# When the stored weight sums, the gathers, the token count and a residual step are issued in a conditioned block

## The chip, the cores and the metric

The kernel runs on one core of one Trainium2 chip. The metric is the device time of one execution in microseconds. A core has five engines with a queue each, which run side by side and wait for one another through semaphores: TensorE (PE in the profile; its weight loads are PEld), VectorE (DVE), ScalarE (ACT), GpSimd (POOL) and SyncE (SP). DMAs are issued from the queues of SP, ACT and POOL. Each queue is in order: what an engine waits for also holds up everything behind it on that engine.

## The reference

32 sequences of 128 tokens with 512 features, a condition vector for each sequence, and a mask. The block is computed in float32:

```python
emb = silu(t) @ ada_w + ada_b                       # per sequence: shift, scale, gate_msa
norm = layernorm(x) * (1 + scale) + shift
norm = where(m, norm, 0)
fwd = gelu(norm @ ssm_w1 + ssm_b1) @ ssm_w2 + ssm_b2
bwd = flip(gelu(flip(norm) @ bwd_w1 + bwd_b1) @ bwd_w2 + bwd_b2)
x = x + gate_msa * where(m, fwd + bwd, 0)           # changes the tokens with m only
ff_ada = silu(t) @ ffada_w + ffada_b                # shift_mlp, scale_mlp, gate_mlp
h = gelu_tanh((layernorm(x) * (1 + scale_mlp) + shift_mlp) @ ff_w1 + ff_b1)
out = x + gate_mlp * (h @ ff_w2 + ff_b2)
```

The mask is true for the tokens behind a sequence's end: between 0 and 32 of the 128 in each sequence. Only those go through the first half (the lines with `ssm` and `bwd`). All 4096 tokens go through the second half (`ff`).

## The kernel before

**First half.** The masked tokens get 512 slots, in four tiles of 128 (`NS`, `NH` = 256). `tokens_of` finds the token of each slot, and POOL gathers its row with an indirect DMA (`gather_slots`, tiles `xc`). A matmul with `pick` spreads the condition's rows over the slots (`slot_part(at, j, ...)`: j is 0 for shift, 1 for scale, 2 for gate). `modulated` normalises, scales and shifts on VectorE; `hidden` is the first matmul with its gelu on ACT, `project` the second. `keep_gate` copies a gate tile from PSUM to SBUF on ACT. `keep_slots` adds the bias, multiplies by the gate and adds the old row (three VectorE operations), and SP stores the 128 rows into `x1_rows` in HBM. Slots 0 and 1 are done in the opening (`h1` with name `s0`). Slots 2 and 3 have one `hidden` (`s1`, L1148) and then a `project` each, with names `s2` and `s3` (L1165, L1166).

**Token count.** L638 to L656 count the masked tokens and set `start_at`, `more_i` and `col_l`. They are read only at the very end, where a loop treats masked tokens that did not fit into the slots.

**Second half.** The 4096 tokens go in `NP` = 4 pairs of two sides, a side having `G` = 4 sequences. `x_of[p]` holds the rows of a pair in four SBUF tiles, loaded by `load_side` on SP. `take_first_half` then lays the results of the first half over the masked rows: one indirect DMA on POOL for each sequence, from `x1_rows` by `slot_i`; rows without a slot are left alone. `Statistics.one` takes mean and variance of one sequence on VectorE, `root` the inverse root on POOL, `normalised` applies both. Side 0 of a pair is then transposed in 32x32 blocks on VectorE and put in place by 16 DMAs from SP and ACT (`turned`), and ACT applies scale and shift (`scaled`). Side 1 of pair 0 is transposed on TensorE instead (`transposed`, called by `turn(k)`): four transpositions into one PSUM bank of `ps_t`, which has two, and four VectorE operations that empty it with scale and shift. The four turns lie between the matmuls of `project(1, ...)` for slots 3.

Both matmuls of the second half are done by Strassen's scheme (in Winograd's form), with products P1 to P7 of blocks, where blocks of weights and tokens are first added or subtracted. `FirstProduct` does that at two levels: the inner sums of the weights, `t_sum[1]` to `t_sum[4]`, are formed by `weight_sums` on VectorE in tiles that are wanted again later, stored into `t_rows` in HBM by `store_weight_sums`, and loaded back for each pair by `load_weights` into the tiles `tw`. Each sum is 896 KB, in two DMAs. `t_sum[1]` lies in the two tiles `spare`, into which `load_side(1, 0, spare)` later loads side 0 of pair 1; `t_sum[3]` lies in the tile that next holds the normalised rows of side 0; `t_sum[4]` lies where the sums of the token blocks (`TokenBlocks.one`) are formed next.

**Order.** All of this stands in a `manual_schedule`: each engine runs its instructions in the order in which the code issues them, and only the waits are added. Around the change the order is: slots 0 and 1, store of the sums 3, 1, 2 (L620), the modulation of the second half with its transposition `modT` (L623 to L635), token count, sum 4 and its store (L664, L665), load of side 0 of pair 1 (L1128), six gathers (L1131), the copy of the gate rows to HBM on POOL (L1133), statistics and root of side 0, two gathers, normalisation and `turned`, statistics and root of side 1, slots 2, slots 3 with the four turns, and then the first products with their block sums.

Of the kernel before, what the change touches and what calls it, by code (L numbers as in the profile page):

```python
# [9 lines left out]
F32 = mybir.dt.float32  # L10
I32 = mybir.dt.int32
# [3 lines left out]
ALU = mybir.AluOpType  # L15
# [7 lines left out]
def kernel(  # L23
# [49 lines left out]
    nc = tc.nc  # L73
    B, S, D = x.shape
    P = 128
    assert S == P
    G = 4
# [4 lines left out]
    NS = 512  # L82
    NH = NS // 2
# [6 lines left out]
    const = ctx.enter_context(tc.tile_pool(name="const", bufs=1))  # L90
# [53 lines left out]
    w2 = ssm.tile([P, HC, D], F32, name="w2")  # L144
# [37 lines left out]
    def hidden(xT, n, w, bcol, func, name, pool, parts=range(HC)):  # L182

        h = []
        for f in parts:
            ph = ps_h.tile([P, 512], F32, tag="h", name=f"ph_{name}_{f}")
            for k in range(KC):
                nc.tensor.matmul(  # L188
                    ph[:, :n], w[:, k, ts(f, P)], xT[:, k, :], start=(k == 0), stop=(k == KC - 1)
                )  # L190
            t = pool.tile([P, n], F32, tag="h", name=f"h_{name}_{f}", bufs=HC + 2)
            nc.scalar.activation(t, ph[:, :n], func, bias=biasT[:, bcol + f : bcol + f + 1])  # L192
            h.append(t)
        return h

    def project(i, h, w, name, between=None):

        po = ps_o.tile([P, 512], F32, tag="o", name=f"po_{name}_{i}")
        for f in range(HC):
            if between and f in between:  # L200
                between[f]()
            nc.tensor.matmul(po, h[f][:, ts(i, P)], w[:, f, :], start=(f == 0), stop=(f == HC - 1))  # L202
        return po
# [205 lines left out]
    slot_col = const.tile([P, NC], F32, name="slot_col")  # L409
# [22 lines left out]
    count = const.tile([B, 1], BF16, name="count")  # L432
# [4 lines left out]
    for j in range(2):  # L437
# [4 lines left out]
            start=True,  # L442
            stop=True,
# [139 lines left out]
            }[j]()  # L583
            nc.vector.tensor_tensor(sum_block(j, n), x, y, ALU.subtract)

    def store_weight_sums(*which):
        for j in which:
            nc.sync.dma_start(t_rows[j - 1, :, :4], t_sum[j][0])
            nc.sync.dma_start(t_rows[j - 1, :, 4:], t_sum[j][1][:, :3])


    h1 = []
    gs = []
    xn_s = []
    for c in range(2):
        h1 += hidden(xT_s, NH, w1, 0, AF.Gelu, "s0", ssm, range(4 * c, 4 * c + 3))
        rows = slot_part(2 + c, 1, ps_o, "o"), slot_part(2 + c, 0, ps_o, "o")
        gs.append(keep_gate(c, slot_part(c, 2, ps_o, "o")))
        xn_s.append(modulated(xc[2 + c], *rows, f"s{2 + c}", xn[:, 2 + c]))
        if c == 0:  # L600
# [16 lines left out]
    nc.vector.tensor_scalar(modb_f[B : 2 * B], modb_f[B : 2 * B], 1.0, None, ALU.add)  # L617
    finish_slots(1, h1, gs[1])

    store_weight_sums(3, 1, 2)  # L620

    mod2 = const.tile([3 * B, D], F32, name="mod2")
    pm = ps_o.tile([P, 512], F32, tag="o", name="pm_f")  # L623
# [10 lines left out]
        )  # L634
    nc.vector.tensor_copy(modT.rearrange("p k c -> p (k c)"), ptr[:, : KC * 3 * B])  # L635


    pt = ps_t.tile([P, 512], F32, tag="tr", name="pt")  # L638
    for j in range(2):
        nc.tensor.matmul(pt[:, j : j + 1], every[:, j], count, start=True, stop=True)  # L640
    totals = const.tile([P, 2], F32, name="totals")
    nc.vector.tensor_copy(totals, pt[:, :2])
    total = totals[:, 0:1]
    start_at = const.tile([P, 1], F32, name="start_at")
    nc.vector.tensor_scalar(
        start_at, totals[:, 1:2], float(NH), -float(NS - NH), ALU.is_gt, ALU.mult
    )
    nc.vector.tensor_scalar(start_at, start_at, float(NS), None, ALU.add)
    more_f = const.tile([P, 1], F32, name="more_f")
    nc.vector.tensor_tensor(more_f, total, start_at, ALU.subtract)  # L650
    nc.vector.tensor_scalar(more_f, more_f, float(P - 1), 0.0, ALU.add, ALU.max)
    more_i = const.tile([P, 1], I32, name="more_i")
    nc.vector.tensor_copy(more_i, more_f)
    nc.vector.tensor_scalar(more_i, more_i, 7, None, ALU.logical_shift_right)
    col_l = const.tile([P, 1], F32, name="col_l")
    nc.vector.tensor_scalar(col_l, slot_col[:, 0:1], start_at, None, ALU.add)  # L656

    of_x = {}

    fb2_step = const.tile([P, D // 2], F32, name="fb2_step")  # L660
# [1 line left out]
    t = in_blocks(sp.tile([P, G, D], F32, tag="s12", name="tw_4"))  # L662
    t_sum[4] = [t[:, :4], t[:, 4:]]
    weight_sums(4)  # L664
    store_weight_sums(4)  # L665


    def take_first_half(p, xs, which=range(2 * G)):
        slots = NH if p == 0 else NS
        for i in which:  # L670
            b = 2 * p * G + i
            nc.gpsimd.indirect_dma_start(  # L672
                out=xs[i // G][i % G // 2][:, i % 2],
                out_offset=None,
                in_=x1_rows[:slots, :],
                in_offset=bass.IndirectOffsetOnAxis(ap=slot_i[:, b : b + 1], axis=0),
                bounds_check=slots - 1,
                oob_is_err=False,
            )
# [445 lines left out]
                self.finish(c, 1, 0, a)  # L1125
                self.store(c, 1)

    x_of[1] = [load_side(1, 0, spare)]  # L1128


    take_first_half(0, x_of[0], range(G + 2))  # L1131
    gate_rows = dram.tile([B, D], F32, name="gate_rows")
    nc.gpsimd.dma_start(gate_rows, mod2[2 * B : 3 * B, :])  # L1133
    stats = [Statistics(x_of[0][side], f"0_{side}") for side in range(2)]
    xT = [new_xT(0, side) for side in range(2)]
    for i in range(G):
# [316 lines left out]
```

## Time and profile before

| | us |
|---|---|
| median of 3 runs | 468.26 |
| lowest and highest of them | 466.21, 471.18 |
| the profiled execution | 466.71 |
| its span | 465.0 |
| TensorE busy in it | 449.4 |
| VectorE busy | 331.4 |
| ScalarE busy | 175.0 |
| GpSimd busy | 157.3 |

The granted TensorE clock was 0.998 of full speed. A busy share is a mean over stages with different limits, so it tells little of one place; in the stretch from the first slots' stores (54 us) to the end of the first product's start (114 us) the engines have to be read in order of time. In a line of the timeline the first number is the start in microseconds from the beginning of the span, the second the duration; then come engine, line, operation, output and input. The brackets at the end hold the time for which the engine was idle before it, and what ended that wait. In a table of stretches each engine has its busy microseconds and, in brackets, its instructions; the last columns are the granted clock, the busy share of the 16 DMA engines, and GB/s.

### The profile page before, as it was taken

How to read it: one execution, taken by the hardware profiler on the slowest of the kernel's cores; microseconds unless marked ns; L12 is line 12 of the kernel's file. 1: busy time of each engine (PE TensorE's matmuls, PEld its weight loads, DVE VectorE, ACT ScalarE, POOL GpSimd, SP SyncE). 2: the span in 40 equal slices, each digit the busy share in tenths (PEclk: the TensorE clock that was granted, in tenths of full speed). 3: DMA queues.
4: the chain of work that ended last, by engine and by line, in shares of the span. 5: the costliest groups of instructions: out<-in, count | busy, mean ns of one | idle time of the engine just before them, and what ended most of it. 6: DMA issues, size and time to landing. Idle time of an engine off the chain costs nothing.

```text
span 465.0 us, 5826 instructions
## 1 busy us (share of the span) xinstructions
PE 449.4 (97%) x2000; PEld 364.3 (78%) x2000; DVE 331.4 (71%) x538; ACT 175.0 (38%) x380; POOL 157.3 (34%) x151
## 2 busy tenths in 40 slices
PE   6899998899999999999999999999999999999995
PEld 2475384477888888888888888888888878888884
DVE  4639767899678749986787399867863995434645
ACT  3122020634454371353554613444446144562000
POOL 6200063038972000489710005897000025660000
PEclk9999999999999999999999999999999999999999
DMA  8999893362408653923087348230963342222022
GB/s 277 386 407 355 329 346 68 65 235 64 160 0 209 98 101 100 335 77 147 1 221 105 83 136 320 87 111 3 231 100 78 125 170 78 81 75 107 0 78 107
DMA packets 82482, 70.41 MB, mean 151 GB/s; under 512 B 63168, under 2 KB 63696, under 8 KB 81426
## 3 DMA queue, kind: packets, MB, share of 16 engines
q1 hardware_dynamic: 67586, 57.95, 40.3%
q0 software_dynamic: 4256, 10.75, 6.9%
q10 hardware_dynamic: 10608, 1.32, 2.1%
q8 instruction: 17, 0.28, 0.3%
q14 instruction: 15, 0.12, 0.1%
HBM read 56.83 MB, written 13.17 MB: 151 GB/s over the span
## 4 chain that ended last, share of the span: by engine, by line
PE 63%; DVE 13%; POOL 6%; ACT 6%; issue 6%; SPq 5%; DMA 1%; POOLq 0%; DVEq 0%; ACTq 0%
PE a_m L904 15%; PE a_o L1084 14%; PE e_o L1084 12%; PE e_m L904 12%; SPq L743 5%; PE po_s L202 4%; PE ph_s L188 3%; DVE xn L716 1%; ACT xT L726 1%; ACT hb L866 1%; POOL x L672 1%; DVE sx L833 1%; POOL hb L988 1%; POOL rstd L710 1%; DVE xn_sy L837 1%
## 5 line engine op out<-in xcount | busy, mean ns | idle before, releaser
L955 POOL TENSOR_TENSOR ha<-p_m,ha 128x512 f32<-128x512 f32 x20 | 26.8, 1342 | 152.4 <-ACT ha L962 143.3
L1084 PE MATMUL e_o<-fw,ha 128*128 128x256 f32 x256 | 57.9, 379 | 0.0
L726 ACT ACTIVATE xT<-xT,modT 128x128 f32<-128x128 f32 x112 | 43.8, 480 | 31.4 <-DMA xT<-xn 31.4
L1084 PE MATMUL a_o<-t,hb 128*128 128x256 f32 x240 | 54.1, 379 | 0.0
L1084 PEld LDWEIGHTS e_o<-fw,ha 128*128 128x128 f32 x256 | 48.6, 190 | 6.6
L1084 PEld LDWEIGHTS a_o<-t,hb 128*128 128x128 f32 x240 | 45.6, 190 | 6.2
L672 POOL DMA_INDIRECT x<-x_rows,slot_i x32 | 37.0, 1155 | 26.2 <-DMA x_rows<-t_s 17.9
L866 ACT ACTIVATE hb<-hb,biasT 128x256 f32<-128x256 f32 x64 | 29.0, 501 | 27.8 <-POOL hb L988 19.4
L955 POOL TENSOR_TENSOR hb<-p_m,hb 128x512 f32<-128x512 f32 x20 | 27.7, 1384 | 21.5 <-DVE hb L934 21.1
L918 ACT COPY p_m<-e_m 128x512 f32<-128x512 f32 x27 | 15.8, 586 | 48.2 <-PE e_m L904 45.4
L1084 PE MATMUL e_o<-fw,s 128*128 128x256 f32 x128 | 29.2, 381 | 0.5 <-DVE s L1038 0.3
L962 ACT COPY ha<-e_m 128x512 f32<-128x512 f32 x32 | 18.5, 579 | 29.1 <-PE e_m L904 24.1
L1084 PE MATMUL a_o<-fw,ha 128*128 128x256 f32 x128 | 28.9, 379 | 0.0
L1084 PE MATMUL a_o<-t,s 128*128 128x256 f32 x128 | 28.9, 379 | 0.0
L188 PE MATMUL ph_s<-xT_s,w 128*128 128x256 f32 x128 | 28.7, 382 | 0.0
L202 PE MATMUL po_s<-w,h_s 128*128 128x512 f32 x64 | 28.6, 592 | 0.0
L1084 PEld LDWEIGHTS e_o<-fw,s 128*128 128x128 f32 x128 | 24.1, 190 | 4.8 <-DVE s L1038 1.7
L188 PEld LDWEIGHTS ph_s<-xT_s,w 128*128 128x128 f32 x128 | 24.0, 190 | 4.7 <-ACT h_s L192 1.5
L1084 PEld LDWEIGHTS a_o<-t,s 128*128 128x128 f32 x128 | 24.3, 190 | 3.3
L1084 PEld LDWEIGHTS a_o<-fw,ha 128*128 128x128 f32 x128 | 24.3, 190 | 3.3
L866 ACT ACTIVATE ha<-e_m,biasT 128x256 f32<-128x256 f32 x48 | 20.1, 469 | 15.3 <-PE e_m L904 12.2
L929 DVE TENSOR_TENSOR e_m<-a_m,ha 128x512 f32<-128x512 f32 x20 | 13.9, 697 | 16.1 <-POOL ha L955 6.6
(205 smaller groups left out, 868.8 us busy)
## 6 DMA issues: line engine op xcount, KB each, us to landing
tw<-t_rows SPq DMA_DIRECT2D x16, 896.0 KB, 5.4
x<-in_x_dram SPq DMA_DIRECT2D x16, 512.0 KB, 12.0
gate<-gate_rows POOLq DMA_DIRECT2D x8, 1024.0 KB
out_dram<-x SPq DMA_DIRECT2D x15, 512.0 KB, 3.4
xT<-xn SPq DMA_DIRECT2D x92, 64.0 KB, 2.3
fw<-in_L_cond_ff_w_dram SPq DMA_DIRECT2D x2, 2048.0 KB
ada_f<-in_L_cond_ffada_w_dram SPq DMA_DIRECT2D x4, 768.0 KB
ada_a<-in_L_cond_ada_w_dram SPq DMA_DIRECT2D x4, 512.0 KB, 3.8
```

Source lines behind the costliest of these rows:

```text
L188: nc.tensor.matmul(ph[:, :n], w[:, k, ts(f, P)], xT[:, k, :], start=(k == 0), stop=(k == KC - 1))
L202: nc.tensor.matmul(po, h[f][:, ts(i, P)], w[:, f, :], start=(f == 0), stop=(f == HC - 1))
L672: nc.gpsimd.indirect_dma_start(out=xs[i // G][i % G // 2][:, i % 2], out_offset=None, in_=x1_rows[:slots, :], in_offset=bass.IndirectOffse ...
L726: nc.scalar.activation(out, src, AF.Identity, bias=shift, scale=scale)
L743: queues[b % len(queues)].dma_start(dst[ts(q, R), b], src[ts(b, R), q])
L866: nc.scalar.activation(dst[:, n], src[:, n], AF.Gelu_apprx_tanh, bias=biasT[:, f : f + 1])
L904: nc.tensor.matmul(bank[:, ts(n, QT)], self.w_block(j, product)[:, ts(n, P)], self.x_block(j, product), start=(product in ("P1", "P5") and ...
L918: nc.scalar.copy(p5, e)
L929: nc.vector.tensor_tensor(e, a, p5, add)
L955: nc.gpsimd.tensor_tensor(self.place(RESULT[j], c), self.p5[j], other, ALU.add)
L962: nc.scalar.copy(self.place(RESULT[j], c), src)
L1084: nc.tensor.matmul(part, src[:, k, ts(i, P)], w[product][:, k, :], start=(last and k == 0), stop=True, skip_group_check=True,)
```

## The change

- `store_weight_sums` takes a queue. Only sum 3 is still stored in the old place. Sum 4 is stored from POOL, behind the last gather and the copy of the gate rows; sums 1 and 2 are stored from SP behind the matmuls of slots 3.
- The load of side 0 of pair 1 moves behind the stores of sums 1 and 2.
- Five gathers of pair 0 instead of six stand in front of the first root, and three behind it. The copy of the gate rows moves behind the last gather.
- The token count becomes the function `count_more`, called in the opening behind the first three tiles of `hidden`.
- In the opening the gate of a slot tile is picked and copied before its scale and shift.
- `finish_slots(2)` is taken apart: its `project` stays, and its `keep_slots` goes behind the transpositions and the emptying of turns 0 and 1, in front of turn 2.

```diff
-    def store_weight_sums(*which):
+    def store_weight_sums(*which, queue=nc.sync):
         for j in which:
-            nc.sync.dma_start(t_rows[j - 1, :, :4], t_sum[j][0])
-            nc.sync.dma_start(t_rows[j - 1, :, 4:], t_sum[j][1][:, :3])
+            queue.dma_start(t_rows[j - 1, :, :4], t_sum[j][0])
+            queue.dma_start(t_rows[j - 1, :, 4:], t_sum[j][1][:, :3])
+
+    def count_more():
+
+        pt = ps_t.tile([P, 512], F32, tag="tr", name="pt")
+        for j in range(2):
+            nc.tensor.matmul(pt[:, j : j + 1], every[:, j], count, start=True, stop=True)
...
+        return total, start_at, more_i, col_l
...
         h1 += hidden(xT_s, NH, w1, 0, AF.Gelu, "s0", ssm, range(4 * c, 4 * c + 3))
+        if c == 0:
+            total, start_at, more_i, col_l = count_more()
+        gs.append(keep_gate(c, slot_part(c, 2, ps_o, "o")))
         rows = slot_part(2 + c, 1, ps_o, "o"), slot_part(2 + c, 0, ps_o, "o")
-        gs.append(keep_gate(c, slot_part(c, 2, ps_o, "o")))
...
-    store_weight_sums(3, 1, 2)
+    store_weight_sums(3)
...
-    pt = ps_t.tile([P, 512], F32, tag="tr", name="pt")
...
     weight_sums(4)
-    store_weight_sums(4)
...
-    x_of[1] = [load_side(1, 0, spare)]
-
-
-    take_first_half(0, x_of[0], range(G + 2))
-    gate_rows = dram.tile([B, D], F32, name="gate_rows")
-    nc.gpsimd.dma_start(gate_rows, mod2[2 * B : 3 * B, :])
+
+    take_first_half(0, x_of[0], range(G + 1))
     stats = [Statistics(x_of[0][side], f"0_{side}") for side in range(2)]
     xT = [new_xT(0, side) for side in range(2)]
     for i in range(G):
         stats[0].one(i)
     stats[0].root()
-    take_first_half(0, x_of[0], range(G + 2, 2 * G))
+    take_first_half(0, x_of[0], range(G + 1, 2 * G))
+    gate_rows = dram.tile([B, D], F32, name="gate_rows")
+    nc.gpsimd.dma_start(gate_rows, mod2[2 * B : 3 * B, :])
+    store_weight_sums(4, queue=nc.gpsimd)
...
-    finish_slots(2, h1, gs[0])
-    po = project(1, h1, w2, "s3", {0: turn(0), 1: turn(1), 2: turn(2), 4: turn(3)})
+    po_s2 = project(0, h1, w2, "s2")
+
+    def keep_and_turn():
+        keep_slots(2, po_s2, gs[0])
+        turn(2)()
+
+    po = project(1, h1, w2, "s3", {0: turn(0), 1: turn(1), 2: keep_and_turn, 4: turn(3)})
+    store_weight_sums(1, 2)
+    x_of[1] = [load_side(1, 0, spare)]
     of_x[0] = TokenBlocks(0, xT)
     of_x[0].one(1)
```

More of the change, by code (lines that the diff above doesn't have):

```diff
@@ L584, in weight_sums @@
             nc.vector.tensor_tensor(sum_block(j, n), x, y, ALU.subtract)
-    def store_weight_sums(*which):
+    def store_weight_sums(*which, queue=nc.sync):
         for j in which:
-            nc.sync.dma_start(t_rows[j - 1, :, :4], t_sum[j][0])
-            nc.sync.dma_start(t_rows[j - 1, :, 4:], t_sum[j][1][:, :3])
+            queue.dma_start(t_rows[j - 1, :, :4], t_sum[j][0])
[4 more added lines that the diff above has]
+            nc.tensor.matmul(pt[:, j : j + 1], every[:, j], count, start=True, stop=True)
+        totals = const.tile([P, 2], F32, name="totals")
+        nc.vector.tensor_copy(totals, pt[:, :2])
+        total = totals[:, 0:1]
+        start_at = const.tile([P, 1], F32, name="start_at")
+        nc.vector.tensor_scalar(
+            start_at, totals[:, 1:2], float(NH), -float(NS - NH), ALU.is_gt, ALU.mult
+        )
+        nc.vector.tensor_scalar(start_at, start_at, float(NS), None, ALU.add)
+        more_f = const.tile([P, 1], F32, name="more_f")
+        nc.vector.tensor_tensor(more_f, total, start_at, ALU.subtract)
+        nc.vector.tensor_scalar(more_f, more_f, float(P - 1), 0.0, ALU.add, ALU.max)
+        more_i = const.tile([P, 1], I32, name="more_i")
+        nc.vector.tensor_copy(more_i, more_f)
+        nc.vector.tensor_scalar(more_i, more_i, 7, None, ALU.logical_shift_right)
+        col_l = const.tile([P, 1], F32, name="col_l")
+        nc.vector.tensor_scalar(col_l, slot_col[:, 0:1], start_at, None, ALU.add)
+        return total, start_at, more_i, col_l
     h1 = []
@@ L635 @@
     nc.vector.tensor_copy(modT.rearrange("p k c -> p (k c)"), ptr[:, : KC * 3 * B])
-    pt = ps_t.tile([P, 512], F32, tag="tr", name="pt")
[L639 to L656, printed above, removed]
     of_x = {}
```

## The prediction

> **What bounds the kernel now.** I read the chain that ended last first, then the busy time by stretch, then the timeline of 54 to 114 us, where every moved instruction but the token count starts. The chain, by engine:
>
> ```profile
> PE 63%; DVE 13%; POOL 6%; ACT 6%; issue 6%; SPq 5%; DMA 1%; POOLq 0%; DVEq 0%; ACTq 0%
> ```
>
> TensorE carries it, but not everywhere. Busy time in three stretches (columns: stretch, sum, PE, PEld, DVE, ACT, POOL, clock, DMA share, GB/s):
>
> ```profile
> 72.30:79.40 7.10, 7.10 (x18) 2.91 (x16) 6.50 (x15) 0.47 (x1) 1.25 (x2) 1.00 0.31 47
> 79.40:92.00 12.60, 9.84 (x35) 4.98 (x35) 10.42 (x25) 7.75 (x18) 0.81 (x1) 1.00 0.46 79
> 92.00:113.40 21.40, 20.31 (x89) 15.80 (x87) 20.75 (x31) 9.58 (x19) 11.19 (x9) 1.00 0.44 158
> ```
>
> TensorE is full to 79.4, loses 2.76 us up to 92, and from 92 to 113.4 VectorE is full (20.75 of 21.40) and TensorE follows it; after 113.4 TensorE is full again. The change can therefore pay only through the holes of 79.4 to 92. The timeline says what makes them (start, duration, engine, line, operation, and in brackets the idle time before and its end):
>
> ```profile
> 57.62 1.08 POOL L672 DMA_INDIRECT x<-x_rows,slot_i  x1 [17.88 <-DMA x_rows<-t_s]
> ...
> 63.54 0.69 DVE L704 BATCH_NORM_STATS2 st<-x 128x6 f32<-128x512 f32 x1 [0.81 <-DMA x<-x_rows,slot_i]
> ...
> 68.40 0.69 DVE L704 BATCH_NORM_STATS2 st<-x 128x6 f32<-128x512 f32 x1 [1.00 <-DMA x<-x_rows,slot_i]
> ...
> 69.60 1.05 POOL L710 TENSOR_TENSOR rstd<-ve,half 128x4 f32<-128x4 f32 x1 [2.79 <-DVE ve L709]
> ...
> 80.25 1.92 DVE L716 TENSOR_SCALAR xn<-x,mv,rstd 128x512 f32<-128x512 f32 x4 [1.17 <-POOL rstd L710]
> ...
> 80.94 1.61 PE L732 MATMUL ptr<-ident,xn 128*128 128x128 f32 x4 [1.52 <-DVE xn L716]
> ...
> 82.08 0.68 DVE L208 TENSOR_TENSOR t_s<-po_s,b 128x512 f32<-128x512 f32 x1
> ...
> 84.20 3.91 DVE L724 TENSOR_SCALAR xT<-ptr,modT 128x128 f32<-128x128 f32 x12
> ...
> 85.62 0.66 PE L732 MATMUL ptr<-ident,xn 128*128 128x128 f32 x4 [0.92 <-DVE xT L724]
> ...
> 91.91 0.69 DVE L208 TENSOR_TENSOR t_s<-po_s,b 128x512 f32<-128x512 f32 x1 [0.81 <-PE po_s L202]
> ```
>
> Two waits of TensorE: for the normalised tiles (80.94) and for a free transposition bank (85.62), which the three `keep_slots(2)` operations (82.08 to 84.28) hold up on VectorE. Back from 80.25 the chain is the root, the statistics and the landing of the gathers: the fourth was issued at 61.84 to 63.60 and read only at 68.40. Why they land late, from the DMA columns, beside the stores queued then:
>
> ```profile
> 58.00:60.00 2.00, 2.00 (x13) 1.71 (x13) 1.38 (x7) 0.55 (x1) 1.70 (x2) 1.00 1.03 396
> 62.00:64.00 2.00, 2.00 (x11) 1.74 (x11) 1.19 (x2) 0.52 (x2) 1.70 (x2) 1.00 1.01 368
> 72.00:74.00 2.00, 2.00 (x7) 1.10 (x6) 1.93 (x4) 0.47 (x1) 1.23 (x2) 1.00 0.03 5
> ```
>
> ```profile
> 56.09 0.97 SPq L588 DMA_DIRECT2D t_rows<-x  x1
> ...
> 96.79 0.80 SPq L850 DMA_DIRECT2D tw<-t_rows  x2
> ```
>
> The DMA engines are saturated (share about 1, near 390 GB/s) from 56 to 70 us. The stored sums are not read before 96.79.
>
> **What the Trainium skill says.** "DMA: Bandwidth & Descriptors", Issuing engines are not separate DMA queues: transfers of SP, ACT and POOL interleave on the same 16 engines. The trace agrees: four gathers of POOL land 4.8 to 4.95 us after their issue ended, beside SP's stores. The same page, Anatomy of one DMA — SWDGE (gpsimd) path: about 2.0 us fixed plus bytes / 436e3. The trace has 2.02 us for a 256 KB store into x1_rows at 54.74, in a gap of the traffic (110 GB/s). "SBUF — State Buffer", SBUF: two separate sides: VectorE with two SBUF inputs and GpSimd exclude each other for a whole instruction. The trace fits: two `sx` adds at 100.35 took 1.53 and 1.75 us beside POOL's L955, against 0.68 elsewhere.
>
> **The change part by part.**
>
> *Count and gate rows in the opening.* Two small matmuls (0.20 us) go from 58.34 to about 26.6; TensorE is full in both places, so net nothing. The eight VectorE operations (58.92 to 60.33, 1.4 us) go to about 26.8, where VectorE waits 6.22 us for the slot gathers until 29.06. Price 0; without that cover, 1.4 us on `modulated`. The gate copy on ACT is 0.7 us earlier, and ACT waits there for TensorE: 0. On VectorE `weight_sums(4)` now ends at 61.3 instead of 62.7, earlier than the second gather lands.
>
> *Stores 1, 2, 4 and side 0 of x_of[1] leave the gathers' traffic.* At 390 GB/s (the saturated rows) one sum of 896 KB is 2.35 us of DMA; three and the 1 MB load are 9.7 us out of the 14 saturated ones. Only sum 3 stays ahead, drained by about 58.5. I price a gather's landing at 2.0 us after its issue; bounds 1.0 (estimate: half of that) and 4.9 (as now). The fourth: 63.60 + 2.0 = 65.6 instead of 68.40, so the root starts at 65.6 + 1.2 (68.40 to 69.60, as now) = 66.8, 2.8 us earlier. Five gathers are issued by 64.9, so POOL waits for VectorE, not the reverse. Behind the waiting root stand three gathers, the gate_rows DMA and sum 4's two DMAs: gathers 1.0 to 1.4 us each with 0.3 between (68.0 to 72.0), the rest about 0.6 each, POOL done at about 74. The gathered rows are read by statistics from 72.8 on, the last at 75.2, and the last gather lands at 74.0. The second root is due at 76.4. Price 0; each 1 us beyond these margins would cost up to 1.
>
> *From the root to TensorE.* Root to last `xn_b` takes 12.57 us (69.60 to 82.17), so `xn_b` is done at 79.4. `project(0)` ends at 79.4 as before: the 1.5 us wait and the gaps in the first transposition go, and TensorE becomes the limit. An even faster landing brings nothing more.
>
> *keep_slots(2) behind the second transposition.* From 79.95 (TensorE's first four transpositions, 0.6) VectorE runs without a hole: evictions of turn 0 and 1 (2 x 1.3), keep (2.2), turns 2 and 3 (2.6), `one(1)` 1.2 = 8.6, to 88.55. TensorE's banks are free in time (turn 2 asks at 82.0, bank 0 is empty at 81.25; turn 3 at 84.2, bank 1 at 82.55), and project s3 ends near 88.1. The first add of `keep_slots(3)`, on which the VectorE-bound stretch hangs, starts at 88.55 instead of 91.91: **3.35 us**. Its own part: with gathers as late as now, moving keep alone gives 0.7 us (evictions from 82.5, same sum, 91.2).
>
> *Turned transfers, ACT and sum 4.* SP's blocks may start at 72.9, ACT's only after its last gelu, 73.06 instead of 75.72. From there to the first `scaled` took 9.81 us, and 16 `scaled` 6.26: done at 89.1 instead of 91.8, just ahead of `seed(1)` at 89.3. Sum 4's 2.35 us of DMA now fall at about 73 to 75.5 beside these blocks, whose DMA share is 0.9 to 1.0. Cost between 0 and 2.35 us of landing; up to 0.2 hidden, the rest passed through ACT's seed and P6 to VectorE, whose idle 0.61 at 96.81 hides some: 0 to 1.4 in the end. I take 0.4.
>
> *SP behind project s3.* keep_slots(2)'s store at 84.8, four stores (0.4 to 1.2 us each) to 87-89.4, the side-0 load waiting for sum 1 to land (about 90), its two DMAs to 91.5. Queued behind: keep_slots(3)'s store (due 92.85) and the `tw` loads (due 93.4). Sum 2 lands near 92. All in time; 0. Bounds 0 and, at congested prices, 4 (below). Nothing is gained by issuing these later.
>
> Sum: -3.35 + 0.4 + 0.1 (rounding of the root's margin) = **-2.85 us**. From 113.4 on only shifts. The profiled execution was 466.71 (span 465.0 and 1.7 around it): 463.9. The median of the runs, 468.26, lies 1.55 above it, and gives 465.4; I write the middle, 464.6.
>
> **Rivals.** *The gain is mostly spent on the turned transfers* (or the gathers land no faster): for it speaks the full DMA share at 78 to 84, against it that about half of sum 4 would drain while the blocks are still being issued. Gain 0.7 to 1.4: about 465.7 to 467.5 by the two bases. *Slower: the sums come back too late.* SP is in order, and a store now precedes its own reading by 8 us instead of 40. With issue at 1.05 us mean (0.97, 0.93, 1.19, 1.11 now), landing 6.4 (the longest of now) and the side-0 load's 2.7 us of traffic ahead, sum 2 lands at 95.8, and the first `tw` at 95.8 + 5.2 + 2.7 = 103.7, against 102.97, the first matmul that reads it today: +0.7, and up to +3 if the second load misses its matmul too; 468.5. It decides from a landing after 99.6, and turns the sign from 102.97. Against it: the DMA engines are idle (0 to 8 GB/s) from 86 to 96 today, so congested prices should not hold. *A larger gain*: the two `sx` adds no longer meet POOL's adds, 1.8 us more: 462.5. Both follow the same VectorE results, so I doubt it.
>
> **Chances.** Forecast 0.60, small gain 0.18, slower 0.12, larger 0.10. Range 461.0 to 468.0: from the larger gain on the profiled run's basis to just short of the slower case. A measurement of this kernel tells about 1% (4.7 us) from no change; the forecast is 0.6%. Faster by over 1%: the larger gain and a quarter of the forecast, 0.25; slower by over 1%: the worse half of the slower case and what I have missed, 0.09; the rest 0.66.
>
> **What would show it.** Right: first statistics without a DMA wait near 61.5; root near 66.8; no wait at the bank; TensorE without idle from 79.4 to 88; first `keep_slots(3)` add near 88.6; everything after 113.4 shifted alike. Wrong: gathers still 4 us or more to landing; `scaled` starting after 84; an SP wait for `t_rows` before the `tw` loads and TensorE idle before its first `tw` matmul.

## The result, and the profile after

| us | before | after |
|---|---|---|
| median | 468.01 (12 runs, 465.86 to 471.18) | 465.73 (12 runs, 464.79 to 467.79) |
| profiled execution, its span | 466.71, 465.0 | 467.79, 466.0 |
| TensorE clock in it | 0.998 | 0.995 |

The ratio of the changed kernel to the kernel before is 0.996, with an interval of 0.9936 to 0.9984: about 1.9 us less; the two medians differ by 2.3. The profiled execution of the changed kernel happens to be the slowest of its twelve, and TensorE's clock was halved for a while in it, so it is read here beside a second profiled execution of the same kernel (label after_again, span 464.7, clock 0.999).

The chain of the changed kernel that ended last, by engine. SP's part, 5% before, is gone from it:

```profile
PE 74%; POOL 8%; ACT 5%; issue 5%; DVE 4%; DMA 3%; SPq 0%; POOLq 0%; DVEq 0%
```

The changed kernel in three of the stretches shown of before (columns as there). In the last two lines, where the gathers are issued, the DMA share was about 1 before; now it is 0.70, and then 0.09:

```profile
79.40:92.00 12.60, 11.14 (x42) 6.01 (x40) 11.92 (x26) 7.88 (x19) 0.00 (x0) 1.00 0.84 229
58.00:60.00 2.00, 2.00 (x11) 1.20 (x10) 0.72 (x2) 1.12 (x2) 1.24 (x2) 1.00 0.70 277
62.00:64.00 2.00, 2.00 (x11) 1.77 (x10) 1.79 (x5) 0.47 (x1) 1.70 (x2) 1.00 0.09 18
```

TensorE's loss between 79.4 and 92 fell from 2.76 us to 1.46, not to nothing. The timeline of the changed kernel, to be laid beside that of before, with the lines between left out (L675 is L672 of before; all line numbers from there on are three higher):

```profile
58.45 1.08 POOL L675 DMA_INDIRECT x<-x_rows,slot_i  x1 [18.58 <-DMA x_rows<-t_s]
62.16 0.69 DVE L707 BATCH_NORM_STATS2 st<-x 128x6 f32<-128x512 f32 x1
66.09 0.69 DVE L707 BATCH_NORM_STATS2 st<-x 128x6 f32<-128x512 f32 x1 [0.23 <-DMA x<-x_rows,slot_i]
67.30 1.05 POOL L713 TENSOR_TENSOR rstd<-ve,half 128x4 f32<-128x4 f32 x1 [1.57 <-DVE ve L712]
79.79 0.60 PE L735 MATMUL ptr<-ident,xn 128*128 128x128 f32 x4
88.94 0.68 DVE L208 TENSOR_TENSOR t_s<-po_s,b 128x512 f32<-128x512 f32 x1
92.40 1.59 PE L907 MATMUL e_m<-xT,fw 128*128 128x256 f32 x4 [1.52 <-ACT e_m L953]
97.05 0.70 DVE L932 TENSOR_TENSOR e_m<-a_m_alone,p_m 128x512 f32<-128x512 f32 x1 [3.83 <-PE a_m_alone L907]
```

Down to 88.94 this is what was forecast: gathers land at once, the root is 2.3 us earlier, TensorE has no wait for `xn` and none for a bank, `keep_slots(3)` (the line at 88.94) starts 3 us earlier. Then comes a new wait: TensorE for 1.52 us on ACT's seed, the copy with which the sum in `e_m` begins (L953). The two groups of four matmuls behind it take 1.59 and 1.91 us instead of 1.03, since the granted clock was 0.73 from 92 to 94 and 0.50 from 94 to 96. VectorE starts `e_m` of L932 at 97.05; before it was at 96.81:

```profile
96.81 0.70 DVE L929 TENSOR_TENSOR e_m<-a_m_alone,p_m 128x512 f32<-128x512 f32 x1 [0.61 <-ACT p_m L918]
```

So the 3 us won at `keep_slots(3)` were spent within 8 us. In after_again, where the clock stayed at 1.00, about 1.8 us of them are left at this place (part A of the ledger below). Who was late is seen on ACT's queue. Before:

```profile
75.72 7.09 ACTq L743 DMA_DIRECT2D xT<-xn  x8
85.53 6.26 ACT L726 ACTIVATE xT<-xT,modT 128x128 f32<-128x128 f32 x16 [1.20 <-DMA xT<-xn]
```

After:

```profile
73.49 10.31 ACTq L746 DMA_DIRECT2D xT<-xn  x8
85.60 6.26 ACT L729 ACTIVATE xT<-xT,modT 128x128 f32<-128x128 f32 x16 [0.27 <-DMA xT<-xn]
91.77 0.57 ACT L953 COPY e_m<-a_m_alone 128x512 f32<-128x512 f32 x1
```

ACT's eight turned blocks start 2.2 us earlier and take 3.2 us longer to issue; `scaled` starts where it did, ends where it did, and the seed behind it now comes too late for a TensorE that is early.

**A ledger for all runs.** The start of `project` `s2` on TensorE differs between two executions of one kernel (72.39 and 73.09 before) nearly as much as between all kernels (72.34 to 73.15). Measured from there, the execution falls into three parts: *A* up to VectorE's first `e_m` of L932 (L929), *B* from there to the first matmul of L1087 (L1084), and the rest. From the timelines, in us:

| kernel | s2 starts | scaled starts | A | B | rest |
|---|---|---|---|---|---|
| before, two executions | 72.39, 73.09 | 85.53, 86.23 | 24.42, 24.72 | 37.38, 37.39 | 330.8, 329.8 |
| after, two executions | 72.93, 73.15 | 85.60, 86.13 | 24.12, 22.74 | 38.56, 38.57 | 330.4, 330.2 |
| sum4_early | 72.96 | 83.57 | 20.92 | 37.37 | 329.7 |
| sum4_early_spread | 72.85 | 83.53 | 20.92 | 38.46 | 330.8 |
| sum4_twice | 72.66 | 92.32 | 30.91 | 37.40 | 330.4 |
| keep_back | 72.85 | 89.52 | 29.06 | 38.57 | 330.6 |
| keep_and_sums12_back | 72.34 | 90.31 | 30.23 | 38.58 | 331.1 |
| keep_back_gated | 73.14 | 86.91 | 23.52 | 44.20 | 329.6 |
| keep_back_held | 73.07 | 85.59 | 22.28 | 38.58 | 330.2 |
| sums12_back | 72.56 | 86.85 | 24.05 | 38.58 | 330.1 |
| count_gate_back | 72.55 | 84.38 | 21.59 | 38.58 | 329.9 |
| keep_alone | 72.63 | 85.82 | 24.98 | 37.38 | 330.0 |

Part A is the stretch on which the prediction worked. Part B is 37.4 or close to 38.6 everywhere but in keep_back_gated, and it takes 1.19 us of the gain away again in the changed kernel. (The parts A and B have nothing to do with the theories A and B of the expectations below.)

### The profile page after: what moved, and what is told of

Its sections match the earlier page's. It is cut to its first block, busy times and chain, and to the rows that moved or that the text cites. A ratio compares the mean times of both kernels' runs of the same rounds, so it can differ in the third digit from the quotient of the medians.

```text
span 466.0 us, 5828 instructions
## 1 busy us (share of the span) xinstructions
PE 451.4 (97%) x2000; PEld 365.3 (78%) x2000; DVE 330.8 (71%) x538; ACT 175.4 (38%) x380; POOL 160.0 (34%) x153
## 4 chain that ended last, share of the span: by engine, by line
PE 74%; POOL 8%; ACT 5%; issue 5%; DVE 4%; DMA 3%; SPq 0%; POOLq 0%; DVEq 0%
PE a_o L1087 19%; PE e_o L1087 16%; PE a_m L907 14%; PE e_m L907 11%; PE ph_s L188 6%; PE po_s L202 4%; POOL hb L991 2%; ACT hb L869 2%; POOL x L675 2%; DMA x<-in_x_dram 2%; DMA tw<-t_rows 1%; POOL ha L958 1%; DVE xT L727 1%; ACT ha L869 1%; PE part_s L283 1%
## 5 line engine op out<-in xcount | busy, mean ns | idle before, releaser
L1087 PE MATMUL e_o<-fw,ha 128*128 128x256 f32 x256 | 57.9, 379 | 0.0
L1087 PE MATMUL a_o<-t,hb 128*128 128x256 f32 x240 | 54.1, 379 | 0.0
L1087 PEld LDWEIGHTS e_o<-fw,ha 128*128 128x128 f32 x256 | 48.6, 190 | 6.6
L1087 PEld LDWEIGHTS a_o<-t,hb 128*128 128x128 f32 x240 | 45.6, 190 | 6.2
L675 POOL DMA_INDIRECT x<-x_rows,slot_i x32 | 37.5, 1173 | 26.9 <-DMA x_rows<-t_s 18.6
L1087 PE MATMUL e_o<-fw,s 128*128 128x256 f32 x128 | 29.2, 381 | 0.5 <-DVE s L1041 0.3
L1087 PE MATMUL a_o<-fw,ha 128*128 128x256 f32 x128 | 28.9, 379 | 0.0
L1087 PE MATMUL a_o<-t,s 128*128 128x256 f32 x128 | 28.9, 379 | 0.0
L1087 PEld LDWEIGHTS e_o<-fw,s 128*128 128x128 f32 x128 | 24.1, 190 | 4.8 <-DVE s L1041 1.7
L1087 PEld LDWEIGHTS a_o<-t,s 128*128 128x128 f32 x128 | 24.3, 190 | 3.3
L1087 PEld LDWEIGHTS a_o<-fw,ha 128*128 128x128 f32 x128 | 24.3, 190 | 3.3
L932 DVE TENSOR_TENSOR e_m<-a_m,ha 128x512 f32<-128x512 f32 x20 | 13.9, 696 | 17.6 <-POOL ha L958 7.4
```

Of the source, the lines that this page charges most:

```text
L675: nc.gpsimd.indirect_dma_start(out=xs[i // G][i % G // 2][:, i % 2], out_offset=None, in_=x1_rows[:slots, :], in_offset=bass.IndirectOffse ...
L932: nc.vector.tensor_tensor(e, a, p5, add)
L1087: nc.tensor.matmul(part, src[:, k, ts(i, P)], w[product][:, k, :], start=(last and k == 0), stop=True, skip_group_check=True,)
```

## The experiments

Ratios are to the kernel before in the same set of runs (medians 467.68, 467.08, 467.46 and 467.77 us in the four sets).

**after_again.** The changed kernel once more.

> The changed kernel as it is, for a second profile in which TensorE's clock is not reduced between 92 and 98 us. Both theories: about 0.996 of the kernel before. Theory A (sum 4's DMAs beside the turned blocks spend part of the gain): the 8 blocks of ACT's queue take about 10 us again instead of 7.1, `scaled` starts at about the time of the kernel before, and VectorE has a hole of 1.5 us or more before its add into e_m (L932). Theory B (the gain is lost behind 88 us, in SP's queue with the stores of sums 1 and 2 ahead of the tw loads): TensorE waits before its first matmul with tw.

Measured: 466.14 us (22 runs), ratio 0.997 (0.9958 to 0.9982). The interval lies below 1, so the small gain is real. The blocks of ACT's queue took 10.13 us to issue and VectorE idled for 2.06 us before L932, as theory A said; no matmul waited for `tw`, against theory B. Here the clock stayed at 1.00 behind a wait of 1.45 us, and A was 22.74.

**sum4_early.** Sum 4 goes from POOL directly behind the fifth gather, in front of the first root, instead of behind the last gather.

```diff
     take_first_half(0, x_of[0], range(G + 1))
+    store_weight_sums(4, queue=nc.gpsimd)
...
     nc.gpsimd.dma_start(gate_rows, mod2[2 * B : 3 * B, :])
-    store_weight_sums(4, queue=nc.gpsimd)
```

> Sum 4 is stored from POOL behind the fifth gather and in front of the first root, when the DMA engines are idle, and not behind the gate rows. Theory A: ACT's 8 blocks take about 7 us, `scaled` starts 9.8 us after ACT's last gelu (2.5 us earlier than in the changed kernel), VectorE's hole at L932 shrinks to under 1 us, and the time falls by 1.2 to 1.9 us against the changed kernel: 0.992 to 0.9935 of the kernel before. Theory B: no difference to the changed kernel, 0.996. If POOL's two DMA issues delay the root, up to 1 us slower than theory A says.

Measured: 462.8 us (6 runs), ratio 0.9907 (0.9886 to 0.9929): faster than both kernels. The issue of the blocks from ACT's queue and ACT's `scaled` in sum4_early:

```profile
73.56 8.22 ACTq L746 DMA_DIRECT2D xT<-xn  x8
83.57 6.26 ACT L729 ACTIVATE xT<-xT,modT 128x128 f32<-128x128 f32 x16 [0.27 <-DMA xT<-xn]
```

The blocks start as in the changed kernel and are issued in 8.22 us instead of 10.31; `scaled` starts 2.0 us earlier, TensorE's wait for the seed is gone, and A is 20.92. The root stays at 67.30, so the store costs the gathers nothing. Part B is back at 37.37. A and B together are 3.02 us less than in after_again, and the medians differ by 3.34. Theory A had 1.2 to 1.9: A alone gives 1.82, and the return of B was in no expectation.

**sum4_twice.** Sum 4 stored a second time into a scratch tensor behind the first store: twice the traffic.

```diff
     store_weight_sums(4, queue=nc.gpsimd)
+    again = dram.tile([P, 7, 2 * P], F32, name="again")
+    nc.gpsimd.dma_start(again[:, :4], t_sum[4][0])
+    nc.gpsimd.dma_start(again[:, 4:], t_sum[4][1][:, :3])
```

> The changed kernel with sum 4 stored a second time (into a scratch tensor that nobody reads) directly behind the first store, on POOL: twice the traffic of 896 KB beside the turned blocks, nothing else. Theory (sum 4's traffic costs the turned blocks 1.5 to 2 us, about its own 2.35 us of DMA time): scaled starts 1.5 to 2.4 us later than in the changed kernel, at 87.3 to 88.5, and the time rises by 1.0 to 2.5, to 467.2 to 468.7. Rival (the blocks were slow for their many small descriptors, and sum 4 hardly matters; sum4_early gained by POOL's gathers): scaled at 85.6 to 86.2 and 465.7 to 466.6.

Measured: 473.37 us (6 runs), ratio 1.0102 (1.0068 to 1.0137). The direction is the theory's; the loss against the changed kernel, 7.2 us, is almost three times the most that it allowed. SP, ACT and TensorE in sum4_twice:

```profile
73.33 13.02 ACTq L746 DMA_DIRECT2D xT<-xn  x8
92.32 6.29 ACT L729 ACTIVATE xT<-xT,modT 128x128 f32<-128x128 f32 x16 [4.43 <-DMA xT<-xn]
...
85.88 0.49 SPq L588 DMA_DIRECT2D t_rows<-x  x1
...
93.25 2.08 PE L907 MATMUL a_m_alone<-xT,fw 128*128 128x256 f32 x4 [4.91 <-ACT xT L729]
```

The second copy adds 2.7 us to the issue of the blocks, as it should. But then ACT's issue ends only at 86.35, and SP, which has sent the row store of `keep_slots(2)` at 85.27, has begun its stores of sums 1 and 2 at 85.88. `scaled` starts 6 us after the end of the issue instead of 1.8. The trace reads as if the cost had a step: it jumps when one bulk transfer pushes the blocks into the next one. One of the six executions took 468.93 us, near what the theory said, the other five 472.68 to 473.71, which fits; the one has no trace that could show it. Part of the loss is the clock's: TensorE idles 4.91 us and then works at half clock (0.50 from 92 to 102).

**keep_back.** The changed kernel, but `keep_slots(2)` again ahead of the transpositions.

```diff
-    po_s2 = project(0, h1, w2, "s2")
-
-    def keep_and_turn():
-        keep_slots(2, po_s2, gs[0])
-        turn(2)()
-
-    po = project(1, h1, w2, "s3", {0: turn(0), 1: turn(1), 2: keep_and_turn, 4: turn(3)})
+    finish_slots(2, h1, gs[0])
+    po = project(1, h1, w2, "s3", {0: turn(0), 1: turn(1), 2: turn(2), 4: turn(3)})
```

> The changed kernel with keep_slots(2) back in front of the four turns. Theory A: `scaled` on ACT sets the pace of what follows, so the wait for a transposition bank (about 1 us) returns on TensorE and moves the end by 0 to 0.5 us: 0.996 to 0.997. Rival C (moving keep_slots(2) is what made the kernel faster, the gathers' earlier landing being hidden anyway): back to 0.999 to 1.001.

Measured: 471.78 us (6 runs), ratio 1.0094 (1.0072 to 1.0116): 5.6 us more than the changed kernel, and slower than before. Both expectations missed. The bank wait that came back is 0.91 us, far too little. SP, ACT and TensorE in keep_back:

```profile
82.25 0.58 SPq L302 DMA_DIRECT2D x_rows<-t_s  x1
82.88 1.03 SPq L588 DMA_DIRECT2D t_rows<-x  x1
...
73.61 10.29 ACTq L746 DMA_DIRECT2D xT<-xn  x8
...
89.52 6.26 ACT L729 ACTIVATE xT<-xT,modT 128x128 f32<-128x128 f32 x16 [4.10 <-DMA xT<-xn]
...
96.31 2.08 PE L907 MATMUL e_m<-xT,fw 128*128 128x256 f32 x4 [3.19 <-ACT e_m L953]
```

SP stands in its queue behind the row store of `keep_slots(2)`. That comes at 82.25 instead of 85.24, and the stores of sums 1 and 2 follow at 82.88, while ACT issues its blocks until 83.90. `scaled` can start at 89.5 instead of 85.6. In and behind TensorE's wait of 3.19 us the clock was halved for 6.8 us, which is part of the loss.

**keep_and_sums12_back.** keep_back with sums 1 and 2 stored early again, in the old place; the load of side 0 of pair 1 stays behind slots 3.

```diff
-    store_weight_sums(3)
+    store_weight_sums(3, 1, 2)
...
-    store_weight_sums(1, 2)
```

> The changed kernel with both undone: keep_slots(2) in front of the turns, sums 1 and 2 stored with sum 3 ahead of the gathers. Theory D (keep_back lost its 5.9 us because SP, no longer waiting for the later keep_slots(2), put the stores of sums 1 and 2 beside ACT's last turned blocks): without those stores there, keep_slots(2)'s place costs 0 to 1 us against sums12_back (0.9994): 0.9994 to 1.0015. Rival E (the loss is the wait for a transposition bank on TensorE): the loss stays, 1.010 to 1.013.

Measured: 472.91 us (5 runs), ratio 1.0126 (1.0099 to 1.0152): no recovery. Taken alone this speaks against the stores of sums 1 and 2 as the cause. The trace says why it didn't tell: with the stores gone, the side-0 load, 1 MB, stood behind the row store instead, at 83.79, before ACT's issue ended at 84.64, and `scaled` waited 4.14 us. It needs nothing of that load, but the profile puts the end of the wait down to it:

```profile
90.31 6.26 ACT L729 ACTIVATE xT<-xT,modT 128x128 f32<-128x128 f32 x16 [4.14 <-DMA x<-in_x_dram]
```

If so, it matters that something large follows, and not which tile it is. That is a reading of one trace; the next two runs test it.

**keep_back_gated.** keep_back, and SP first stores eight floats of the last turned block, so that what follows cannot start sooner.

```diff
+    landed = dram.tile([1, 8], F32, name="landed")
+    nc.sync.dma_start(landed, xT[0][P - 1 : P, KC - 1, G * S - 8 :])
     store_weight_sums(1, 2)
```

> As keep_back (the changed kernel with keep_slots(2) ahead of the transpositions), but SP first issues a store of eight floats of the last turned block, so that the stores of sums 1 and 2 and the side-0 load cannot start before the turned blocks have landed. Theory F (keep_back lost 5.6 us because the early keep_slots(2) let SP's large transfers start at 82.9 beside ACT's last turned blocks, which then landed 4 us late): scaled starts at 85.5 to 87.0 instead of 89.52, TensorE's wait for ACT's seed is 1.5 us or less instead of 3.19, and the time is 466.0 to 468.0 (the bank wait of 0.9 us stays, and the tw loads may come up to 1 us late). Rival G (the order on VectorE costs it: the bank wait and the later evictions of the transpositions): nothing changes but SP, 470.5 to 472.5. A value between, 468.5 to 470, means both.

Measured: 473.14 us (6 runs), ratio 1.0116 (1.0089 to 1.0143). By the time alone the rival (the order on VectorE) would have won; by the trace the run was late for another reason. In this place the small store waits for `scaled` as well, and so until 93.19. SP and TensorE in keep_back_gated:

```profile
93.19 0.25 SPq L1170 DMA_DIRECT2D landed<-xT  x1
...
107.05 2.05 PE L907 MATMUL e_m<-sx,tw 128*128 128x256 f32 x4 [3.84 <-DMA tw<-t_rows]
```

`scaled` did start at 86.91 and A fell from 29.06 to 23.52, but the `tw` loads went out at 100.24, 6.4 us later than in the changed kernel, TensorE waited 3.84 us for them and then worked at half clock for 6.8 us, and B is 44.20 instead of 38.6. This is the mechanism of the prediction's slower rival, brought about by another delay.

**keep_back_held.** The same eight floats, placed directly behind the turned blocks, where only their landing is waited for.

```diff
     turned(xn, xT[0], (nc.sync, nc.scalar))
+    landed = dram.tile([1, 8], F32, name="landed")
+    nc.sync.dma_start(landed, xT[0][P - 1 : P, KC - 1, G * S - 8 :])
```

> keep_back (the changed kernel with keep_slots(2) ahead of the transpositions), with SP's store of eight floats of the last turned block placed directly behind the turned blocks. In keep_back_gated it stood behind scaled in the program and so waited until 93.2 for ACT to have scaled the block, which brought the tw loads 6.4 us late (TensorE waited 3.84 for tw) and hid the answer. Here it waits for the landing alone, so SP's stores should start near 86, as in the changed kernel. Theory F (SP's large transfers beside ACT's last turned blocks cost keep_back its 5.6 us): scaled starts at 85.5 to 87.2, TensorE's wait for ACT's seed is 1.8 us or less, no wait for tw over 1 us, and 466.0 to 468.0. Rival G (the order on VectorE costs it): scaled and the stores as just said, but 470.5 to 472.5.

Measured: 465.5 us (11 runs), ratio 0.9956 (0.9939 to 0.9974), against 471.78 for keep_back; the theory's range was 466.0 to 468.0, the rival's 470.5 to 472.5. SP and ACT in keep_back_held:

```profile
85.55 0.24 SPq L1153 DMA_DIRECT2D landed<-xT  x1
...
86.28 0.42 SPq L588 DMA_DIRECT2D t_rows<-x  x1
...
85.59 6.26 ACT L729 ACTIVATE xT<-xT,modT 128x128 f32<-128x128 f32 x16 [0.26 <-DMA xT<-xn]
```

A store of 32 bytes that does nothing but hold SP takes 6.3 us off. The bank wait of 0.91 us is still there, and `keep_slots(3)` starts at 89.97, 16.90 behind `s2`, where it is 16.01 and 16.40 in the changed kernel; the time is no worse for it. So the theory of SP's traffic holds, and the order on VectorE by itself, here with the other parts of the change, is worth nothing that these runs can see.

**sums12_back.** The changed kernel with sums 1 and 2 stored early (the first part of the diff of keep_and_sums12_back).

> The changed kernel with sums 1 and 2 stored behind sum 3 again, ahead of the gathers. Theory A: the gathers land 4 us or more after their issue, the first root starts near 69 us or later, xn_b is done after 81 us, and the gain falls to that of keep_slots(2) alone or less: 0.998 to 1.000. Theory B: the stores are out of SP's way behind 88 us, so the kernel is as fast as or faster than the changed one, 0.993 to 0.996.

Measured: 466.94 us (22 runs), ratio 0.9994 (0.9978 to 1.001), in theory A's range. Against the 22 runs of after_again in the same set it is 0.8 us more in the median and 1.3 in the mean. The gathers meet more traffic again: the first is read 4.86 us after the end of its issue, the root starts 4.02 us ahead of `s2` (5.63 and 5.17 in the changed kernel, 2.79 before), and A is 24.05. So moving the stores of sums 1 and 2 is worth about 1 us of the 1.5 that the change brought in this set.

**keep_alone.** The kernel before with nothing changed but `keep_slots(2)` behind turns 0 and 1 (the `+` lines of `keep_and_turn` in the change).

> The kernel before with one part of the change: keep_slots(2) behind the first two turns. The sums are stored early as before, so nothing collides with the turned blocks, and `scaled` ends at 91.8 as before, 1 us ahead of the seed that follows it. The forecast's own part for it: 0.7 us faster, 0.998 to 0.999. Rival C (keep_slots(2)'s place is worth the 5.9 us that keep_back lost): 0.987.

Measured: 466.42 us (14 runs), ratio 0.9991 (0.9971 to 1.001): no gain to be seen, though the 0.7 us forecast for it would fit into this interval too. Its trace speaks against it: `keep_slots(3)` starts 20.09 us behind `s2`, where before it was 19.52 and 19.82. The rival's 0.987 is excluded.

**count_gate_back.** The changed kernel with the token count and the order of gate and scale rows as before.

> The changed kernel with the token count and the gate rows back in their old places. Forecast: both cost nothing in either place, so 0.996 to 0.998 like the changed kernel. Rival F (the count's eight VectorE operations in front of the statistics push the first root back, since the gathers now land early): up to 1.4 us slower, 0.998 to 1.000.

Measured: 465.62 us (14 runs), ratio 0.9959 (0.9941 to 0.9976), against 0.997 (0.9958 to 0.9982) for after_again: these two parts of the change bring nothing measurable and cost nothing measurable. No run undoes the place of the sixth gather or that of the copy of the gate rows alone.

**before_again.** The kernel before once more, one profile, for the spread between traces.

> The kernel before as it is, for a second profile. If the changed kernel's later start of the gathers (58.1 to 59.6 us in five profiles, 57.62 in the one of before) comes from the opening's loads and not from the change, the first gather starts anywhere from 57.6 to 59.6 here too; if it is the change, it starts at 57.6 again. POOL's first two adds (L955) take 2.9 to 3.0 us together as in the first profile.

Measured: 466.87 us, span 465.0. It is the second value in the first row of the ledger. The first gather starts at 58.33 here, within the range expected if the change is not the reason. Measured from `s2` it starts 14.76 us ahead, as in the first profile (14.77); in the changed kernel it is 14.48 and 13.53, so that a small part of the later start may be the change's. POOL's first two adds take 2.98 us together, as in the first profile.

**sum4_early_spread.** sum4_early with pair 1's eight gathers at four places of the schedule.

```diff
-                put(2, 6, take_first_half, 1, x_next, range(2 * G))
+                put(2, 6, take_first_half, 1, x_next, range(G + 1))
+                put(3, 4, take_first_half, 1, x_next, range(G + 1, G + 2))
+                put(3, 6, take_first_half, 1, x_next, range(G + 2, G + 3))
+                put(5, 4, take_first_half, 1, x_next, range(G + 3, 2 * G))
```

> sum4_early (462.8) with pair 1's eight gathers spread over later places of the schedule: five at the old place, one each at the third slot's fourth and sixth places, the last two in the fifth slot. If POOL's gathers of pair 1, 11.4 us in one piece, hold up POOL's adds for which VectorE waits (1.4, 0.8 and 0.6 us in the kernel before), the time falls by 0.5 to 2.5, to 460.3 to 462.3. If those waits are covered by TensorE's own work, or the later gathers make pair 1's statistics late, it is 462.5 to 464.5.

Measured: 465.37 us (21 runs), ratio 0.9957 (0.994 to 0.9974), 2.6 us worse than sum4_early and outside both ranges. A is the same 20.92; B is 38.46 instead of 37.37, and the rest 330.8 instead of 329.7. POOL's adds behind the five gathers now start at 108.76, when VectorE is forming sums, and take 1.70 and 1.45 us; in sum4_early they start at 111.63 and take 1.29 each. The VectorE sum of 128x256 that starts beside the first of them, at 109.25, takes 1.49 us instead of 0.41, and B grows by just this, 1.09. By these traces it was not the gathers in one piece that held up what matters; adds that move into VectorE's own additions do.

## Why the prediction was right, and where it was not

465.73 us against 464.6 forecast, in the range, and within 1% as held likeliest. The gain was 1.9 us by the ratio where 2.85 was summed. The number alone says little: the range ended at 468.0, the median of before, and 465.73 lies as well at the edge of the first rival's range (465.7 to 467.5), whose mechanism, a gain spent on the turned transfers, is what the runs showed for about half of it. Of the signs named ahead, all but the last of the right ones came, and so did one of the wrong ones: `scaled` started at 85.60, not before 84. In the sum two terms are mis-sized, the collision and what follows 113.4, and in two places the reasoning was wrong without harm to the number.

- **Count and gate rows, 0.** Right; count_gate_back cannot be told from the changed kernel.
- **Gathers landing 2.0 us after their issue.** Right: the fourth was issued at 63.43 to 64.43 and read at 66.09, 1.66 us behind it, with 0.23 us of waiting. The root came at 67.30 where 66.8 was forecast, and the first gather 0.83 later than in the profile of before. The fixed 2.0 us that the Trainium skill gives in "DMA: Bandwidth & Descriptors", Anatomy of one DMA — SWDGE (gpsimd) path, was a fair price as soon as the queue was empty. The store of 2.02 us that the prediction set beside it is no check of it: it went out on SP's queue, and that section is about POOL's.
- **TensorE without idle from 79.4 to 88.** Right: none from 79.79 to 89.4 but what lies between two matmuls.
- **First add of `keep_slots(3)` 3.35 us earlier.** The number is right: measured from `s2`, the mean of 19.52 and 19.82 fell to that of 16.01 and 16.40, 3.47 us. What hangs on it was wrong. The step said that the VectorE-bound stretch hangs on this add. In the changed kernel VectorE has 2 to 4 us of slack before L932, and the stretch hangs on ACT, whose seed stands behind `scaled`. keep_back_held, with the add 0.7 us later and the same time, agrees.
- **Collision of sum 4 with the turned blocks, 0.4 taken from 0 to 1.4.** This is the mis-sized term. sum4_early takes the collision away and A falls by 1.8 us against after_again and by 3.2 against the profiled execution with the reduced clock; `scaled`, measured from `s2`, starts 2.1 to 2.4 us earlier. The estimate took the store's 2.35 us of DMA time, expected about half of it to drain while the blocks were still being issued, and VectorE's idle time to hide more. But the time of the issue was no cover, since the issue itself grew: 1.9 to 2.1 us were added to it (10.13 and 10.31 us against 8.22), and ACT has no slack behind it: table load, `scaled`, seed follow without a hole. The forecast without this term, -3.25, is near what part A of sum4_early gives against the mean of before (24.57 to 20.92, 3.65), and its 9.81 us from the issue of the blocks to `scaled` are 10.01 there. So the mechanism of the forecast was right, and this term was too small.
- **keep_slots(2)'s own part, 0.7.** Wrong in a way that no number in the sum shows. Alone it brought nothing that can be seen (keep_alone); in the company of the moved stores it is what keeps them off the last blocks, worth 5.6 us (keep_back), and eight floats do the same (keep_back_held). The prediction listed the stores behind `keep_slots(2)`'s row store and costed them at 0 because they were in time for `tw`; it did not ask what they would meet if they came sooner. That the change held them back far enough was luck for the forecast.
- **SP behind slots 3, 0.** Right: the `tw` loads went out at 93.82, 0.4 later than forecast, and no matmul waited for them. The rival's mechanism exists, and keep_back_gated priced it: loads 6.4 us later, 3.84 us of TensorE.
- **After 113.4 only shifts.** Wrong by 1.19 us. Part B is 37.4 us in the kernel before and 38.6 in the changed one. The first of two adds on POOL behind VectorE's `hb`, the last gather of pair 1 behind them, and the `e_m` of VectorE that needs POOL's next add; before, and then in the changed kernel:

```profile
100.06 1.27 POOL L955 TENSOR_TENSOR hb<-p_m,hb 128x512 f32<-128x512 f32 x1 [19.85 <-DVE hb L934]
...
113.55 1.00 POOL L672 DMA_INDIRECT x<-x_rows,slot_i  x1 [0.30 <-issue]
...
116.24 0.70 DVE L929 TENSOR_TENSOR e_m<-a_m,ha 128x512 f32<-128x512 f32 x1
```

```profile
100.67 1.72 POOL L958 TENSOR_TENSOR hb<-p_m,hb 128x512 f32<-128x512 f32 x1 [22.70 <-DVE e_m L951]
...
115.31 0.99 POOL L675 DMA_INDIRECT x<-x_rows,slot_i  x1 [0.30 <-issue]
...
117.64 0.70 DVE L932 TENSOR_TENSOR e_m<-a_m,ha 128x512 f32<-128x512 f32 x1 [0.86 <-POOL ha L958]
```

The first add starts 0.23 us behind VectorE's `hb` in the one case and 0.6 in the other, and takes 1.27 or 1.72 us. Pair 1's last gather is issued 16.74 us behind the first `e_m` of L929 before and 18.26 behind that of L932 after, POOL's add behind it is late by as much, and VectorE, which had not waited for it, waits 0.86 us. "SBUF — State Buffer" of the Trainium skill, Who interferes with whom, says that issue order decides who blocks, and the traces fit: in the short case POOL is ahead of VectorE's `sx` add, in the long one VectorE's add has begun. All twelve kernels start this add in one of the two ways, and B lies within 0.02 us of 37.38 or 38.57 accordingly, except in the two where something else was moved in that stretch (keep_back_gated, sum4_early_spread). No run changes this start alone. What moves POOL's start by those 0.4 us is open: sum4_twice has the short form and the changed kernel the long one, though only two DMAs on POOL lie between them. So a larger gain from `sx` adds that no longer meet POOL's was doubted with reason, but that the meeting could get worse was not asked.
- **Slips of the arithmetic.** Gains of 0.7 to 1.4 us below the two bases are 465.3 to 467.6, not 465.7 to 467.5, and 1.8 us below 464.6 is 462.8, not 462.5 (462.1 on the profiled run's basis, where the range has 461.0). From 56 to 68 us the saturated rows of before carry 294 to 401 GB/s, 360 on average, where 390 was used; the 2.35 us of one sum would be 2.55. The forecast's own sum is added up rightly.

Of the sum, then: -3.65 without the collision, +1.8 for the collision, +1.2 for POOL, which is -0.6 by the profiles of before and after_again, where the medians of the two comparisons give -1.5 to -2.3. Single executions of one kernel lie up to 1.4 apart in A and 1.0 in the rest, so that the difference of 0.9 to 1.7 us stays open. That the total came so near the forecast is in part luck: by the profiles alone it was missed by more than 2 us.

## What to carry to other kernels

Bulk transfers that nobody waits for still have to be placed by what they meet: list, for the time in which they would run, the small transfers on other queues that somebody does wait for. Before an instruction with slack is moved, ask what stands behind it in its queue and what that would then collide with; where only the holding is wanted, a tiny store that reads the right tile gives it, if it is issued ahead of what rewrites that tile. And where a stretch looks bound by one engine, look how late the next one is: here ACT had waited only 0.98 us for TensorE ahead of its seed (L950, in the profile of before), so that 3 us taken from TensorE and VectorE could bring little more than that until ACT moved as well.

## What the runs showed of the hardware

- One 896 KB store on POOL's queue lengthened the issue of eight small-piece transfers on ACT's queue from 8.2 and 8.3 us (sum4_early, sum4_early_spread) to between 9.2 and 10.5 (eight traces), and two such stores to 13.0. The stores of sums 1 and 2 or the 1 MB load, begun on SP's queue before the end of this issue, moved the start of `scaled`, counted from that end, from 1.8 to 2.7 us (eleven traces) to 5.6 to 6.0 (keep_back, keep_and_sums12_back, sum4_twice). "DMA: Bandwidth & Descriptors" of the Trainium skill, Queues, rings and completion order, has each DMA engine take its queues in turn, a packet at a time; the traces agree in that the eight blocks on SP's queue were lengthened by as much (6.29 to 8.43 us). What the store itself lost is not shown.
- TensorE's clock fell to 0.50 with short waits. They were 1.52 us (the profiled execution of the changed kernel, 3.4 us at the lower clock), 3.19 (keep_back and keep_and_sums12_back, 6.8 us), 3.84 (keep_back_gated, 6.8 us), and 4.91 with 2.11 (sum4_twice, 10.2 us); a wait of 1.45 us in after_again had no such sequel. The lengths, worked out from the granted clock in stretches of 0.4 us, are one, two and three times 3.4 us. "TensorE: Matmul & The Clock Gate" of the Trainium skill, HAM oscillation — how this bites in real kernels, puts the limit at gaps above some 3.4 us; here 1.5 was enough once. In keep_back the clock is part of the loss: measured from `s2`, `scaled` came 3.7 to 4.0 us late, and A grew by 6.3 against after_again.
- A POOL add and a VectorE sum that met slowed each other: 1.70 us for the one and 1.49 for the other in sum4_early_spread, where they take 1.29 and 0.41 apart (sum4_early).
